# GpSimd instead of ScalarE issues layer 2's weight loads, and the fusion MLPs' inputs are fetched two images ahead: a four-layer convolution stack on one core

## The chip, the cores and the metric

The kernel runs on one core of one Trainium2 chip, in one launch. The metric is the device time of one execution in microseconds (us), given as the median of several runs. TensorE (PE), VectorE (DVE), ScalarE (ACT), GpSimd (POOL) and SyncE (SP) each run their own instructions in order; SP, ScalarE and GpSimd also issue the transfers between the DRAM and the core's own memory.

## The reference

The input x has 8 images of 384 channels of 32 x 32 pixels, float32. Four residual layers follow each other, each on a group-normalised x:

```python
x = x + L0(gn(x))   # convolutional attention: depthwise 3x3, batch norm, gelu, 8 heads
x = x + L1(gn(x))   # 4 experts of two 384x384 layers, 2 of them per pixel
x = x + L2(gn(x))   # depthwise 7x7 with reflected borders
x = x + L3(gn(x))   # three branches of MLPs and depthwise 1x1, 3x3, 5x5, mixed and projected
```

The change touches layer 2 and the beginning of layer 3. Layer 2 is one depthwise convolution:

```python
xp = jnp.pad(x, ((0, 0), (0, 0), (P, P), (P, P)), mode='reflect')     # P = 3
out = jax.lax.conv_general_dilated(xp, w, ..., feature_group_count=C) # w is (384, 1, 7, 7)
return out + b[None, :, None, None]
```

In layer 3, two of four groups of channels in each branch go through a small MLP: `h = gelu(einsum('bchw,cd->bdhw', c, mw1) + mb1)`, `y = einsum('bdhw,dc->bchw', h, mw2) + mb2`. The means of the hidden values over the image are needed for the weights that mix the three branches (the fusion).

## The kernel before, in words

**Layer 2's order of work.** The 384 channels form three tiles (ct = 0, 1, 2). A tile's input, all 8 images, lies in one buffer xt (L1836 fetches it, image by image, on SP's queue). The 7x7 convolution is done by TensorE as products with banded matrices: for each of eight column pairs c and both halves e of one, `convolve7` (L1112, L1116) runs over seven taps. So there are 48 units of work, 28 products each; the trace shows two records for each product. Every second c, ScalarE copies four full accumulator banks into `o` (`evict_slots`, L405).

**The weights' way.** The banded weights w7 lie in DRAM as 24 blocks, one for each tile and column pair (128 rows of 4256 bytes, 532 KB). `load_weights` (L1693) issues the transfer of the next block (L1704) and then two additions on GpSimd (L1708) that fold the reflected border into the band. `next_weights` (L1713) lets ScalarE spread half a block into a `wx` buffer (two activations, L1725), one half for each unit, and, when a block is used up, calls `load_weights`. Blocks land in four buffers, two tagged `w` and two tagged `xn2`; there are three `wx` buffers. `next_weights` is called right after each unit, and the order in which each engine gets its instructions is the order of the calls: the stage is scheduled by hand (`manual_schedule`). So the transfer of a block stood in ScalarE's instruction stream between the spreading of one half and the eviction or spreading that comes next. Four blocks (0, 1, 5 and 6) are issued by SP, the other 20 by ScalarE. The smaller weights of layer 3 (w35, w33) take the same way, without additions.

**Finishing a tile.** When a tile has been evicted, `finish_all` (L1874) has VectorE transpose the 8 images back (L1847), the first four into a buffer x1 and the others into four buffers y, add bias and the residual r that SP fetches (L1850, L1852), take statistics and sums, and SP store the result (L1855). For tiles 0 and 1 GpSimd copies the edges of each image (L1869). GpSimd's stream holds these copies between the additions of L1708, in the order of the calls. Near the end of tile 2 (c = 5), `fetch3` (L1905) has SP read back the stored results into the y buffers, and layer 3's first weights are loaded.

**Counting transfers.** The kernel is built by a framework that places every semaphore. In the built program SP's and ScalarE's transfers together count on eight semaphores (DMAHW0 to DMAHW7) in turn, GpSimd's on eight others (DMASW0 to DMASW7). A transfer whose semaphore was last used by a transfer that is not known to have landed waits for it before it is issued.

**Layer 3's hidden MLPs.** `hidden3(i)` (L2158) handles images 2i and 2i + 1: it takes the two input halves of each image from `hidden_in`, or calls `hidden_input` (L1928), which has GpSimd fetch them into two of the four y buffers (L1931); VectorE scales the weights (L2165), TensorE multiplies (L2171), ScalarE applies the gelu (L2179). `hidden_in` is filled for images 0 and 1 (L2070). Behind `hidden3(0)` stand GpSimd's fetches of the fusion's weights (L2190, L2191) and `windows()`, in which GpSimd fills `count` by 25 memsets (L2120) and VectorE uses it (L2138) ahead of `mean` (L2155). `hidden3(1)` to `hidden3(3)` are called between steps of the 5x5 convolution (L1969).

Of the kernel before, what the change touches and what calls it, by code (L numbers as in the profile page):

```python
# [19 lines left out]
B, C, H, W = 8, 384, 32, 32  # L20
# [33 lines left out]
K7, R7 = 7, 3  # L54
# [121 lines left out]
def conv_mixer_kernel(ctx: ExitStack, tc: tile.TileContext, a: dict, out: bass.AP):  # L176
    nc = tc.nc
# [415 lines left out]
    def layers(again, early, xst, pre_pool, pp0, pw):  # L593
# [531 lines left out]
        def begin_layer2(n, er):  # L1125

            late["xa"] = own.enter_context(
                tc.tile_pool(name="xa", bufs=1, side="right", reuse_waits="tile")
            )
            for name, bufs in (("lw", 2), ("lwx", 1), ("wx", 2)):  # L1130
                late[name] = lwpool.enter_context(
                    tc.tile_pool(name=name, bufs=bufs, side="right", reuse_waits="tile")
                )
            wxs.extend((late["lwx"], late["wx"]))
            fourth.append(er.tile([P, 2 * K7, 2, W], FP, tag="wx", name="wx4", bufs=1))
            xts.append(new_xt(late["xa"]))
            for i in range(n):
                nc.sync.dma_start(out=image_of(xts[0], i), in_=x2mem[i][0])
            for _ in range(2):
                load_weights(nc.sync)  # L1140
# [549 lines left out]
        todo_load = [(K7, ct, c) for ct in range(NC) for c in range(8)]  # L1690
        todo_load += [(n, unit, c) for unit in (1, 0) for n in KS for c in range(8)]

        def load_weights(queue=nc.scalar):  # L1693
            if not todo_load:
                return
            k, unit, c = todo_load.pop(0)
            rows, cols = 4 * k, W + (len(EDGE) if k == K7 else 0)
            n_loaded.append(c)
            if k == K7 and more_w and (len(n_loaded) - 4) % 4 > 1:
                w = more_w[0]()  # L1700
            else:
                w = late["lw"].tile([P, 4 * K7, W + len(EDGE)], FP, tag="w", name="w")
            w = w.rearrange("p r w -> p (r w)")[:, : rows * cols].rearrange("p (r w) -> p r w", w=cols)
            queue.dma_start(out=w, in_=a["w7" if k == K7 else f"w3{k}"][unit, c])  # L1704
            if k == K7:
                for c0, e0 in ((0, W), (W - R7, W + R7)):
                    o = w[:, :, c0 : c0 + R7]
                    nc.gpsimd.tensor_tensor(out=o, in0=o, in1=w[:, :, e0 : e0 + R7], op=ALU.add)  # L1708
            n = rows // WPARTS[k]
            for e in range(WPARTS[k]):  # L1710
                loaded.append(((k, unit, c, e), w[:, n * e : n * e + n, :W]))

        def next_weights():  # L1713
            if not loaded:
                return
            key, w = loaded.pop(0)
            n = w.shape[1]
            n_spread.append(key)
            if len(n_spread) == 4:
                x = fourth.pop()  # L1720
            else:
                m = len(n_spread) - (len(n_spread) > 4)
                x = wxs[m % 3 != 1].tile([P, 2 * K7, 2, W], FP, tag="wx", name="wx")
            for t in range(2):
                nc.scalar.activation(x[:, :n, t, :], w, AF.Copy, scale=parity[:, t : t + 1])  # L1725
            weights[key] = x.rearrange("p r t w -> p r (t w)")
            if key[3] == WPARTS[key[0]] - 1:
                n_placed.append(key)

                if len(n_loaded) - len(n_placed) < (4 if todo_load and todo_load[0][0] == K7 and more_w else 2):  # L1730
                    load_weights()
# [61 lines left out]
        for _ in range(2):  # L1793
            load_weights(nc.sync)
# [3 lines left out]
        def banks(turn=True):  # L1798
            return Slot(four_banks(turn))
# [38 lines left out]
        def new_y():  # L1838
            return ty.tile([P, N], FP, tag="y", name="y", bufs=4)
# [88 lines left out]
        def hidden_input(b):  # L1928
            ys = [new_y() for _ in range(2)]
            for j in range(2):  # L1930
                nc.gpsimd.dma_start(out=ys[j], in_=y2mem[b][1 + j])  # L1931
            return ys
# [57 lines left out]
        with tc.manual_schedule(engines=ORDERED | {mybir.EngineType.Pool}):  # L1990
# [79 lines left out]
            hidden_in = {b: hidden_input(b) for b in range(2)}  # L2070
# [87 lines left out]
            def hidden3(i):  # L2158


                slot, units = banks(i == 0), []
                for b in (2 * i, 2 * i + 1):
                    ys = hidden_in.pop(b, None) or hidden_input(b)
                    mw1s = fa.tile([P, 2, MR], FP, tag="mw1s", name="mw1s", bufs=2)
                    nc.vector.tensor_mul(  # L2165
                        mw1s, mw1, s3[:, 1:3, b : b + 1].to_broadcast([P, 2, MR])
                    )
                    for h in range(2):
                        ph = slot.tile([MR, HF])
                        for j in range(2):  # L2170
                            nc.tensor.matmul(  # L2171
                                ph, lhsT=mw1s[:, j], rhs=ys[j][:, h * HF : (h + 1) * HF],
                                start=j == 0, stop=j == 1,
                            )
                        units.append(ph)
                for b in (2 * i, 2 * i + 1):
                    hid = ty.tile([MR, N], FP, tag="r2", name="hid")
                    for h in range(2):
                        nc.scalar.activation(  # L2179
                            hid[:, h * HF : (h + 1) * HF], units.pop(0), AF.Gelu,  # L2180
                            bias=hbias[:, b : b + 1], accum_out=hsum[:, b, h : h + 1],
                        )
                    nc.scalar.dma_start(out=hmem[b], in_=hid)

            hidden3(0)

            fws = new_x1().rearrange("p c b h -> p (c b h)")
# [96 lines left out]
            def output_bias():  # L2284
                po = banks().tile([P, NC, B])
                for oc in range(NC):
# [8 lines left out]
                convolve3(0, 5, lambda: to.tile([P, B, H, 32], FP, tag="o", name="o")),  # L2295
                [
                    lambda: hidden3(1), None, lambda: hidden3(2), None, lambda: hidden3(3),
                    reorder, branch_mean, branch_weights,
                ],
# [272 lines left out]
```

## Time and profile before

| what | value |
|---|---|
| median of 3 runs | 3133.1 us (3128.01, 3133.1, 3138.59) |
| the profiled execution | 3131.1 us, its span 3129.4 us |
| mean granted TensorE clock | 0.979 of full speed |
| TensorE matmul / weight load busy | 95% / 55% |
| VectorE / ScalarE / GpSimd busy | 59% / 39% / 27% |
| moved by the DMA engines | 323.03 MB, 103 GB/s in the mean |
| layer 2's convolution on TensorE (L1116) | 2625.7 to 2817 us from the span's start |
| layer 3's hidden MLPs on TensorE (L2171) | 2883.9 to 2934.5 us |

Times in the profile are counted from the span's start. A row of a timeline gives start, duration, engine, line, operation, output and inputs, how many instructions are merged, and in brackets how long the engine was idle before it and what ended that. A row of the list of waits gives who waited for whom, the sum in us, how often, and the longest. L numbers are lines of the kernel before; behind L1703 the changed kernel's are one to three higher.

### The profile page before, as it was taken

What the parts mean: (1) busy time and instruction counts of PE and PEld (TensorE: products, weight loads), DVE (VectorE), ACT (ScalarE), POOL (GpSimd) and SP (SyncE); (2) the same over time, 40 slices, a digit from 0 to 9 for tenths busy, and PEclk for the clock granted to TensorE, in tenths of its full rate; (3) what the DMA queues carried; (4) which work ended last, traced back from release to release, by engine and by line L of the source; (5) the groups of instructions that cost most, each with busy time, mean ns of one, the idle gap of its engine ahead of it and who ended that gap; (6) DMA issues with size and microseconds to landing.
All of it is one profiled execution on the core that took longest, in us unless ns stands there. A gap on an engine that the chain in (4) does not pass through costs nothing. (4 is left out here: it accounts for less than half of the span.)

```text
span 3129.4 us, 45250 instructions
## 1 busy us (share of the span) xinstructions
PE 2978.0 (95%) x18280; PEld 1710.8 (55%) x18280; DVE 1857.4 (59%) x3066; ACT 1211.5 (39%) x1446; POOL 858.7 (27%) x1103
## 2 busy tenths in 40 slices
PE   4988999999999999999999999999999999886998
PEld 3765334343433434343433688788787877555543
DVE  6898344445454445444445777777777776457164
ACT  2655453544445353545433122222222223446520
POOL 2432000000000000000000577686777764111400
PEclk9999999999999999999999999999999999898999
DMA  6787102010111101110002111112112114967675
GB/s 220 262 281 287 57 23 83 23 63 23 61 46 41 63 23 63 44 63 23 31 23 94 74 41 65 57 49 85 45 45 81 52 37 161 335 204 251 232 227 187
DMA packets 89107, 323.03 MB, mean 103 GB/s; under 512 B 13608, under 2 KB 16000, under 8 KB 84664
## 3 DMA queue, kind: packets, MB, share of 16 engines
q1 hardware_dynamic: 64936, 251.71, 23.6%
q10 hardware_dynamic: 13776, 35.82, 3.7%
q0 software_dynamic: 10176, 32.51, 3.0%
q8 instruction: 146, 2.39, 0.3%
q14 instruction: 73, 0.60, 0.1%
HBM read 211.66 MB, written 111.68 MB: 103 GB/s over the span
## 5 line engine op out<-in xcount | busy, mean ns | idle before, releaser
L780 ACT ACTIVATE e<-sc 128x1024 f32<-128x1024 f32 x512 | 483.2, 1031 | 607.8 <-PE sc L773 607.7
L773 PE MATMUL sc<-qT,kT 64*128 64x512 f32 x2048 | 473.9, 602 | 0.0
L792 PE MATMUL av<-e,vT 128*64 128x512 f32 x2048 | 467.7, 599 | 0.0
L773 PEld LDWEIGHTS sc<-qT,kT 64*128 64x128 f32 x2048 | 186.8, 186 | 282.0 <-issue 231.3
L792 PEld LDWEIGHTS av<-e,vT 128*64 128x64 f32 x2048 | 135.5, 136 | 316.4 <-issue 316.4
L822 POOL DMA_DIRECT2D att<-att x45 | 23.7, 531 | 979.6 <-DVE att L817 979.6
L671 PE MATMUL sc<-y,pw 128*128 128x512 f32 x576 | 249.3, 594 | 0.0
L808 DVE LOAD_MASK_SELECT sm<-av x64 | 0.9, 14 | 417.0 <-PE av L792 417.0
L530 PE MATMUL ps<-xt,wx 64*64 64x256 f32 x3456 | 198.7, 388 | 35.2 <-DVE xt L468 20.1
L810 DVE RECIPROCAL inv<-sm 128x512 f32<-128x512 f32 x64 | 214.6, 3353 | 2.2
L1346 POOL TENSOR_TENSOR hs_sum<-hs,hs_sum 128x256 f32<-128x256 f32 (+1 forms) x225 | 209.7, 940 | 9.4
L1366 DVE TENSOR_TENSOR r<-r,p 128x256 f32<-128x256 f32 x416 | 153.2, 411 | 92.2 <-PE p L1357 90.7
L530 PEld LDWEIGHTS ps<-xt,wx 64*64 64x64 f32 x3456 | 156.8, 137 | 76.1 <-issue 39.7
L671 PEld LDWEIGHTS sc<-y,pw 128*128 128x128 f32 x576 | 108.8, 190 | 139.9 <-issue 138.5
L354 ACT ACTIVATE hs<-hs,b 128x512 f32<-128x512 f32 x135 | 88.4, 712 | 247.4 <-DVE hs L1308 246.8
L1116 PE MATMUL ps<-xt,wx 64*64 64x256 f32 (+1 forms) x2912 | 160.5, 379 | 23.8 <-ACT wx L1725 12.8
L1357 PE MATMUL p<-hs_sum,wsum 128*128 128x256 f32 x768 | 177.0, 384 | 0.0
L1308 DVE TENSOR_TENSOR hs<-p,hs_sum 128x256 f32<-128x256 f32 x270 | 114.5, 424 | 93.5 <-PE p L1299 39.0
L1299 PE MATMUL p<-forms,w 128*128 128x256 f32 x630 | 165.4, 379 | 0.0
L1323 PE MATMUL ph<-xn,w 128*128 128x512 f32 x342 | 159.3, 600 | 3.0 <-ACT xn L354 3.0
L1357 PEld LDWEIGHTS p<-hs_sum,wsum 128*128 128x128 f32 x768 | 149.2, 194 | 21.4
L1116 PEld LDWEIGHTS ps<-xt,wx 64*64 64x64 f32 x2912 | 109.2, 139 | 73.3 <-ACT wx L1725 15.1
(346 smaller groups left out, 4687.3 us busy)
## 6 DMA issues: line engine op xcount, KB each, us to landing
raw<-y SPq DMA_DIRECT2D x72, 512.0 KB
y<-raw SPq DMA_DIRECT2D x24, 1536.0 KB
x<-x SPq DMA_DIRECT2D x23, 608.0 KB
xt<-x SPq DMA_DIRECT2D x23, 608.0 KB
w<-in_w ACTq DMA_DIRECT2D x36, 384.0 KB
xn<-in_x SPq DMA_DIRECT2D x24, 512.0 KB
x<-in_x SPq DMA_DIRECT2D x16, 768.0 KB
z<-z POOLq DMA_DIRECT2D x16, 768.0 KB, 4.3
```

Of the source, the lines that this page charges most:

```text
L530: nc.tensor.matmul(ps[64 * d : 64 * d + 64, 2 * i + e, cc], lhsT=w[r, 12 * cc + 6 * e + 3 * d + k, :], rhs=xt0s[ct][r, 16 * d + 4 * u + 2 ...
L671: nc.tensor.matmul(ps[:, h, :], lhsT=w[:, ct, pair, :], rhs=y[:, ct, h * HF : (h + 1) * HF], start=ct == 0, stop=ct == NC - 1,)
L773: nc.tensor.matmul(sc[:, s, :], lhsT=kTs[b][r, pair, m * P : (m + 1) * P], rhs=qTs[b][r, pair, h * HF : (h + 1) * HF], start=True, stop=True,)
L780: nc.scalar.activation(e, sc, AF.Exp, scale=1.0 if shifted else HD**-0.5)
L792: nc.tensor.matmul(av[64 * s : 64 * s + 64, :], lhsT=vTs[0][:, m, c0 : c0 + 64], rhs=e[:, s, :], start=m == 0, stop=m == N // P - 1,)
L810: nc.vector.reciprocal(inv, sm)
L1116: nc.tensor.matmul(ps[64 * d : 64 * d + 64, 2 * i + e, c % 2, images], lhsT=w[r, d * K7 + k, :], rhs=by_slot(xts[ct])[r, 16 * d + column(c ...
L1299: nc.tensor.matmul(ps[:, :QF], lhsT=block1(PRODUCTS[n][0])[:, e], rhs=form_of(n, xn), start=True, stop=True,)
L1323: nc.tensor.matmul(ph, lhsT=w1[:, e, ct, dc * P : (dc + 1) * P], rhs=xn[:, ct, :], start=ct == 0, stop=ct == NC - 1,)
L1346: eng.tensor_add(rows_of(o, hs, s), rows_of(i, hs, s), rows_of(j, hs, s))
L1357: nc.tensor.matmul(ps[:, :QF], lhsT=block(w)[:, e], rhs=rows_of(x, hs, e), start=e == 0, stop=e == E - 1,)
L1366: nc.vector.tensor_tensor(out=o, in0=o, in1=ps[:, :QF], op=op)
```

## The change

Every w7 block that ScalarE loaded is now loaded by GpSimd; those that name SP keep it, and layer 3's weights stay with ScalarE. And after the products of image b, the inputs of image b + 2 are fetched at once, instead of at the beginning of the next call of `hidden3`.

```diff
-        def load_weights(queue=nc.scalar):
+        def load_weights(queue=None):
...
             w = w.rearrange("p r w -> p (r w)")[:, : rows * cols].rearrange("p (r w) -> p r w", w=cols)
+            queue = queue or (nc.gpsimd if k == K7 else nc.scalar)
             queue.dma_start(out=w, in_=a["w7" if k == K7 else f"w3{k}"][unit, c])
...
                 for b in (2 * i, 2 * i + 1):
-                    ys = hidden_in.pop(b, None) or hidden_input(b)
+                    ys = hidden_in.pop(b)
...
                         units.append(ph)
+                    if b + 2 < B:
+                        hidden_in[b + 2] = hidden_input(b + 2)
```

On GpSimd each of the 20 transfers now stands directly ahead of its own two additions, with one exception: block 7's stands ahead of the additions of block 6. The issue waits for ScalarE's spreading of the block that held the buffer before. The semaphores of SP's and ScalarE's remaining transfers are dealt out anew, since 20 of them left the round. The first fetch of images 2 and 3 on GpSimd moves ahead of L2190, L2191 and the memsets of L2120; the other orders stay.

## The prediction

> **What bounds the kernel now.** I read the page first. TensorE is busy nearly throughout, but the DMA row jumps to 9 in one slice, at about 2660 to 2740 us.
>
> ```profile
> PE 2978.0 (95%) x18280; PEld 1710.8 (55%) x18280; DVE 1857.4 (59%) x3066; ACT 1211.5 (39%) x1446; POOL 858.7 (27%) x1103
> ...
> DMA  6787102010111101110002111112112114967675
> ```
>
> That stretch is layer 2, whose stage runs from 2637 to 2817 us. The list of waits, cut to 2600 to 2820 us, says who waited there:
>
> ```profile
> ACT wx L1725 <- DMA r<-r: 17.5, 2, 9.1
> ...
> PE ps L1116 <- ACT wx L1725: 12.8, 5, 4.6
> ...
> ACT wx L1725 <- DMA y<-x: 11.1, 1, 11.1
> ACT wx L1725 <- DMA y<-y: 10.9, 1, 10.9
> ACT wx L1725 <- DMA fb<-in_fb: 10.2, 1, 10.2
> PE ps L1116 <- ACT o L405: 9.7, 1, 9.7
> ```
>
> ScalarE waited 17.5 + 11.1 + 10.9 + 10.2 = 49.7 us for four kinds of transfer that SP issues and that L1725 doesn't read. The timeline of ScalarE shows where one such wait sits:
>
> ```profile
> 2662.47 0.33 ACTq L1704 DMA_DIRECT2D xn<-in_w  x1
> ...
> 2667.64 1.23 ACT L1725 ACTIVATE wx<-xn,parity 128x448 f32<-128x448 f32 x2 [2.08 <-PE ps L1116]
> 2678.56 0.33 ACTq L1704 DMA_DIRECT2D xn<-in_w  x1
> 2679.02 1.23 ACT L1725 ACTIVATE wx<-w,parity 128x448 f32<-128x448 f32 x2 [10.15 <-DMA fb<-in_fb]
> ```
>
> The idle time lies ahead of a weight load (L1704 at 2678.56), not ahead of the spreading (L1725) it is booked to. In the built kernel's instruction list the reason is plain: the transfers of SP and ScalarE share eight counters in turn, and this load must first see the SP transfer ahead of it on its counter land. So ScalarE stands, the weights spread behind the load come late, and TensorE runs dry:
>
> ```profile
> 2664.27 12.51 PE L1116 MATMUL ps<-xt,wx 64*64 64x256 f32 x224
> 2680.30 33.71 PE L1116 MATMUL ps<-xt,wx 64*64 64x256 f32 x560 [3.52 <-ACT wx L1725]
> ...
> 2718.57 8.78 PE L1116 MATMUL ps<-xt,wx 64*64 64x256 f32 x112 [4.56 <-ACT wx L1725]
> ...
> 2801.40 5.26 PE L1116 MATMUL ps<-xt,wx 64*64 64x256 f32 x56 [9.73 <-ACT o L405]
> ```
>
> I number the 24 loads of w7 by order (load k holds column pair k % 8 of channel tile k // 8); each is spread in two halves, units 2k and 2k + 1 of TensorE, 56 matmul records each. The row at 2664.27 gives four undisturbed units in 12.51 us, 3.13 us each; the next ten took 3.37 each, and the two from 2718.57 took 4.39, at a granted clock of 0.64 to 0.67 in the slices of 5 us from 2715 to 2725.
>
> **Part one: loads 2 to 4 and 7 to 23 issued by GpSimd.** ScalarE loses 20 issues of 0.33 us and the waits ahead of loads 10, 15, 16 and 23. The fifth stall (10.92 us, to 2797.86) stands before the first w35 load, which stays on ScalarE behind the same SP transfer of fetch3, so it stays too; only its time can move. What lies on the path up to unit 31 (the end of tile 1): idle TensorE of 3.52 + 4.56 + 1.98 us, and slow units of 10 x 0.24 + 2 x 1.26 = 4.9 us; together 15.0 us.
>
> Against it: load 4 now stands behind the copies of L1018 on GpSimd, 0.6 us later than ScalarE's 2645.70; its additions, the memsets of L1081 and the eviction that waits for them follow, and with unit 7 already waiting 0.34 us I take 0.9 us. So unit 31 comes at most 14.1 us earlier.
>
> What is late next? Tile 1's finishing on VectorE must end before fetch3 lands, and fetch3 releases the w35 load, the eviction (L405) behind it and unit 44. Its start, at 2752.83, had two conditions that fell together:
>
> ```profile
> 2751.65 0.75 POOL L1708 TENSOR_TENSOR w<-w 128x84 f32<-128x84 f32 x2 [5.23 <-DMA w<-in_w]
> 2752.34 0.32 POOL L1869 COPY edges<-y 128x8 f32<-128x8 f32 x2
> ```
>
> ```profile
> 2752.83 4.62 DVE L1847 STREAM_TRANSPOSE x<-o 128x1024 f32<-128x1024 f32 x4 [17.84 <-POOL edges L1869]
> ```
>
> The eviction of tile 1 ended at 2752.73. And the last of the eight transposes takes over the y buffer of tile 0's image 7, whose edge copies (L1869, 2752.34) stand on GpSimd behind load 20's additions. That queue is what the change lengthens. Before, a load was in flight while GpSimd waited for an earlier one. Now GpSimd issues a load, waits for it to land, adds (0.75 us), copies edges if due, and only then issues the next; queued behind each landing are the next load, the edge copies, and through them VectorE.
>
> So GpSimd's line has to be added up. Load 7 waits for the spreading that ended at 2654.72, 0.9 us later now; landed and added, it lets load 8 go at about 2660.8. From there to image 7's copies lie thirteen loads, 8 to 20. Nine of them (8 to 16) fall into the saturated stretch, four after it. Landing there: ScalarE's ten loads 9 to 18 took 5.05 to 8.55 us from issue to the additions, 7.0 in the mean (2662.47 to 2671.02 is the longest). GpSimd's own loads of y (512 KB, L1931, at a DMA share of 0.5 to 1.0) landed in 3.8, 5.1 and 7.0 us, lowest, median, highest. I take 6.5: nearer to ScalarE's mean, which is the same transfer in the same stretch, and a little lower because two of mine are never in flight together. In the quiet stretch ScalarE's took 3.7; I take 4.3 for the dearer issue (0.53 against 0.33 us) and y's 3.8 at best. With 0.75 of additions and 0.15 to wake: 9 x 7.4 + 4 x 5.2 + 8 x 0.33 of copies = 90.0 us, so the copies end at 2750.8. One transpose (1.2 us) on, VectorE's L1852 starts at 2752.0 where it started at 2761.88: 9.9 us earlier. The cap of 14.1 would be reached with 6.0 us per landing. The weights themselves stay in time: load 14 would be added at 2660.8 + 7 x 7.4 = 2712.6, and unit 28, at 2654.77 + 0.9 + 21 x 3.13 = 2721.4, needs it a spreading (1.25 us) ahead, at 2720.1.
>
> From there the finishing takes as long as before, less some waits for r (0.88 + 0.75 + 1.85 us), whose SP transfers also lose the loads from their counters; bounds 0 and 3.5, I take 1.0 because VectorE's own work sets most of the pace. Unit 44 and all behind it in layer 3 then come 10.9 us earlier, for that chain (fetch3, w35, eviction, unit 44) keeps its order.
>
> The Trainium skill speaks against a gain of this kind: the page DMA: Bandwidth & Descriptors, section Issuing engines are not separate DMA queues, says that issuing from more engines only saves the sequencer's issue time. By that the sum would be nought for part one, since 20 x 0.33 us of ScalarE are covered; the trace so far disagrees, as the 49.7 us are waits of a queue and no issue time. That case is the third rival.
>
> **Part two: inputs two images ahead.** It does not fetch earlier. In the rows of the trace image 2's loads already wait only for TensorE's reading of image 0 (L2171), because four y buffers hold two images:
>
> ```profile
> 2884.83 0.88 POOL L2120 MEMSET count<- 128x1 f32 x25
> 2887.03 0.54 POOL L1931 DMA_DIRECT2D y<-y  x1 [1.31 <-PE ps L2171]
> ...
> 2890.46 0.53 POOL L1931 DMA_DIRECT2D y<-y  x1 [2.05 <-PE ps L2171]
> ```
>
> ```profile
> 2887.90 0.21 DVE L2138 TENSOR_TENSOR kcount<-ksum,count 128x50 f32<-128x50 f32 x1
> ```
>
> What moves is that L2190, L2191 and the memsets of count (L2120) now stand behind image 3's loads. These end at 2891.85; 1.15 us of issues and 0.88 of memsets put count at 2893.9, where VectorE's L2138 ran at 2887.90. From L2138 to the scaled weights of image 2 (L2165) VectorE needs 2.6 + 0.3 us, so they come at 2896.9, and TensorE's hidden matmuls, which began at 2895.48, wait 1.4 to 1.5 us. TensorE is busy all of 2885 to 2935, so nothing absorbs it: +1.5 us. fw1, also later, isn't read before 2944.
>
> **Sum.** -9.9 - 1.0 + 1.5 = -9.4 us on the profiled execution of 3131.1 us (span 3129.4 and 1.7 around it): 3121.7. The median of the runs is 2.0 higher, so 3123.7 there.
>
> **Rivals.** *GpSimd becomes the pace.* If landings in the saturated stretch take as long as ScalarE's longest or more, the copies, and then the weights, come late. Break-even is at 7.5 us per landing (copies at 2760.2); 8.6 makes it 9.4 us slower, and load 14 would by then be added at 2660.8 + 7 x 9.5 = 2727.3, behind unit 28's need. For it: 8.55, 8.18 and 8.02 us are in the rows, plus 0.2 of dearer issue. Against: the mean is 7.0, with pairs in flight. Price at 9.3 us: 9 x 2.8 = 25 us more on the line than I summed, so +16 us, 3149.
>
> *VectorE holds GpSimd up.* Of GpSimd's additions of 0.40 us a few took 1.37 to 1.40, one at 2701.73 while VectorE ran L1852. If the issue and an addition of the six loads between 2692 and 2735 each lose 0.97 us, the line grows by 11.6 us, and the sum becomes +2.2 us: 3135. Against: the y load issued at 2855.36 during L1852 took 0.63 us where 0.53 is usual. The skill's same page, section SWDGE vs HWDGE vs iDMA, says that the descriptors GpSimd writes lie in SBUF, where VectorE's two-port modes lock it out, and that ScalarE's loads are immune; only the 0.1 us of that row bears it out here.
>
> *The wait moves and nothing is gained.* Only issue time is saved, or the load's wait was for its buffer and is repeated on GpSimd: part one 0, part two +1.5, 3134.6. Against: loads 19 to 22, with the same buffers, issued without such a wait.
>
> **How the numbers follow.** A measurement of this kernel can tell about 0.3%, 9.4 us. My forecast sits on that edge: landings of up to 6.5 us give more, 6.5 to 7.5 less. Forecast (gain of 3 to 16 us) 0.66, of which 0.50 above 9.4; GpSimd the pace 0.18, of which 0.16 beyond +9.4; VectorE 0.09; nothing gained 0.07. Faster 0.50, same 0.34, slower 0.16. The low end is the cap, 14.1 + 3.5 - 1.5 = 16.1 us, less some of the runs' spread (5 us): 3114. The high end takes in a landing of 8.5 us, ScalarE's mean plus 1.5 (9 x 2.0 = 18 us more, so +8.6): 3141.
>
> **What would show it.** Right: the four ScalarE waits of 8 to 11 us ahead of L1705 gone, one left before w35; image 7's copies of tile 0 near 2750; VectorE's second set of transposes ending near 2752; count's memsets at about 8 us after image 0's matmuls. Wrong: w landing in over 7.5 us from GpSimd, TensorE waiting for L1726 in tile 1, or that one remaining stall not ending earlier.

## The result, and the profile after

The changed kernel takes 3125.51 us in the median of 9 runs (3122.39 to 3131.36), the kernel before 3132.43 in 9 runs beside it (3125.64 to 3138.59). The ratio is 0.9982 with a 95% interval of 0.9973 to 0.999: a gain of 5.6 us by the ratio and of 6.9 us between the medians, small, but above nothing by the interval. The span of the profiled execution went from 3129.4 to 3123.3 us. All medians here and below are of undisturbed runs; the kernel before with its first w35 load moved had two more, of 3506.43 and 5527.2 us at a granted clock of 0.846 and 0.708, which are left out.

In what follows, the list of waits is always that of 2600 to 2820 us. In lines of the changed kernel, L1705 is the weight load, L1709 its additions, L1726 the spreading, L1848 the transposes, L1853 bias and residual, L1870 the edge copies.

The page first. TensorE's busy time hardly changes, and in the DMA row the slice of layer 2 has an 8 where the 9 was, and three slices on there is a 7 for a 6:

```profile
PE 2972.1 (95%) x18280; PEld 1719.4 (55%) x18280; DVE 1858.2 (59%) x3066; ACT 1211.7 (39%) x1446; POOL 869.6 (28%) x1123
...
DMA  6787102010111101110002211112112114867775
```

The list of waits of the changed kernel (who waited for whom, sum, times, longest):

```profile
POOL w L1709 <- DMA w<-in_w: 55.6, 14, 7.8
...
ACT wx L1726 <- POOL w L1709: 24.3, 5, 14.2
...
ACT wx L1726 <- DMA y<-y: 19.9, 1, 19.9
...
PE ps L1116 <- ACT o L405: 10.0, 1, 10.0
...
ACT o L405 <- DVE y L1848: 5.3, 1, 5.3
DVE y L1848 <- POOL edges L1870: 4.9, 2, 3.7
...
PE ps L1116 <- ACT wx L1726: 2.7, 1, 2.7
```

Of the four kinds of transfer that held ScalarE up, only y<-y, ahead of the first w35 load, is left (19.9 us, 10.9 before), and TensorE's waits for spread weights fell from 12.8 to 2.7 us. New are two: VectorE waits for edge copies in the middle of its transposes, and ScalarE's eviction for VectorE. And one has grown: ScalarE's spreading waits for GpSimd's additions (w 24.3 us, xn 6.1). Without the first of these waits, which lies ahead of the stage (14.2 us, 14.3 before), that is 16.2 us where it was 1.0.

TensorE's timeline says the same. From 2664.28 on it runs 29 units without a gap, where it had gaps of 3.52, 4.56 and 1.98 us. A unit takes 89.35 / 29 = 3.08 us, and the granted clock, 0.91 from 2660 to 2700 us and 0.87 from 2700 to 2740 us before, is 1.00 in both. So the slow units of the prediction are gone together with the gaps. But unit 44 (2793.08) still stands behind the eviction:

```profile
2664.28 89.35 PE L1116 MATMUL ps<-xt,wx 64*64 64x256 f32 x1624
2756.32 15.58 PE L1116 MATMUL ps<-xt,wx 64*64 64x256 f32 x280 [2.69 <-ACT wx L1726]
...
2781.61 1.45 PE L279 MATMUL ps<-mv,gmatB 128*128 128x8 f32 x6 [9.39 <-DVE mv L1859]
2793.08 6.21 PE L1116 MATMUL ps<-xt,wx 64*64 64x256 f32 x56 [10.02 <-ACT o L405]
...
2813.75 10.74 PE L1970 MATMUL ps<-x,wx 64*64 64x128 f32 x280 [4.11 <-DVE x L1925]
```

GpSimd's line is the one the prediction added up: issue, wait, additions, edge copies, next issue. It reached the copies of image 7 of tile 0 at 2751.65:

```profile
2735.11 0.75 POOL L1709 TENSOR_TENSOR xn<-xn 128x84 f32<-128x84 f32 x2 [5.27 <-DMA xn<-in_w]
...
2746.94 0.56 POOL L1705 DMA_DIRECT2D w<-in_w  x1
2750.96 0.74 POOL L1709 TENSOR_TENSOR w<-w 128x84 f32<-128x84 f32 x2 [3.45 <-DMA w<-in_w]
2751.65 0.31 POOL L1870 COPY edges<-y 128x8 f32<-128x8 f32 x2
```

VectorE's last transpose of tile 1 follows these copies by 0.03 us, and the finishing starts 8.7 us earlier than before (2753.16 for 2761.88):

```profile
2738.97 4.62 DVE L1848 STREAM_TRANSPOSE x<-o 128x1024 f32<-128x1024 f32 x4 [4.87 <-issue]
...
2747.03 1.25 DVE L1848 STREAM_TRANSPOSE y<-o 128x1024 f32<-128x1024 f32 x1 [1.19 <-POOL edges L1870]
2751.99 1.25 DVE L1848 STREAM_TRANSPOSE y<-o 128x1024 f32<-128x1024 f32 x1 [3.72 <-POOL edges L1870]
2753.16 1.24 DVE L1853 SCALAR_TENSOR_TENSOR x<-x,b,r 128x1024 f32<-128x1024 f32 x1
```

ScalarE's timeline holds the two places that matter later. The eviction of tile 1 (2737.03) stands behind a spreading that waited for GpSimd's additions, and the w35 load (2789.54) comes at the end of 19.86 us:

```profile
2735.90 1.23 ACT L1726 ACTIVATE wx<-xn,parity 128x448 f32<-128x448 f32 x2 [4.41 <-POOL xn L1709]
2737.03 1.84 ACT L405 COPY o<-ps 128x2048 f32<-128x2048 f32 x1
...
2789.54 0.33 ACTq L1705 DMA_DIRECT2D w<-in_w  x1
2790.05 1.23 ACT L1726 ACTIVATE wx<-w,parity 128x448 f32<-128x448 f32 x2 [19.86 <-DMA y<-y]
2791.18 1.84 ACT L405 COPY o<-ps 128x2048 f32<-128x2048 f32 x1
```

Part two is seen on GpSimd, VectorE and TensorE. The memsets of `count` come 9.0 us after the first hidden products (2878.46), where they came 0.9 us after them in the kernel before, and TensorE waits ahead of image 2:

```profile
2881.56 0.59 POOL L1932 DMA_DIRECT2D y<-y  x1 [7.01 <-PE ps L2172]
...
2887.43 0.88 POOL L2121 MEMSET count<- 128x1 f32 x25
```

```profile
2888.35 0.21 DVE L2139 TENSOR_TENSOR kcount<-ksum,count 128x50 f32<-128x50 f32 x1 [6.11 <-POOL count L2121]
...
2890.95 0.52 DVE L2166 TENSOR_TENSOR mw1s<-mw,s 128x144 f32<-128x144 f32 x2
```

```profile
2891.36 7.06 PE L2172 MATMUL ps<-y,mw1s 128*72 128x512 f32 x16 [1.27 <-ACT wx L1726]
```

TensorE's row names a spreading of ScalarE, but that had ended at 2890.50. What ended last is VectorE's scaling of the weights (L2166, the first of two, at about 2891.25), and VectorE had stood 6.11 us for `count`.

### The profile page after: what moved, and what is told of

The parts are those of the page before. It is cut to its first block, busy times and chain, and to the rows that moved or that the text cites. A ratio compares the mean times of both kernels' runs of the same rounds, so it can differ in the third digit from the quotient of the medians.

```text
span 3123.3 us, 45274 instructions
## 1 busy us (share of the span) xinstructions
PE 2972.1 (95%) x18280; PEld 1719.4 (55%) x18280; DVE 1858.2 (59%) x3066; ACT 1211.7 (39%) x1446; POOL 869.6 (28%) x1123
## 3 DMA queue, kind: packets, MB, share of 16 engines
q8 instruction: 146, 2.39, 0.3%
## 5 line engine op out<-in xcount | busy, mean ns | idle before, releaser
L530 PEld LDWEIGHTS ps<-xt,wx 64*64 64x64 f32 x3456 | 158.6, 139 | 74.1 <-issue 39.3
L1116 PE MATMUL ps<-xt,wx 64*64 64x256 f32 (+1 forms) x2912 | 153.8, 369 | 13.9 <-ACT o L405 10.0
L1346 POOL TENSOR_TENSOR hs_sum<-hs 128x256 f32<-128x256 f32 (+1 forms) x135 | 132.8, 1013 | 58.7 <-ACT hs L354 50.5
```

The source lines that it names most:

```text
L530: nc.tensor.matmul(ps[64 * d : 64 * d + 64, 2 * i + e, cc], lhsT=w[r, 12 * cc + 6 * e + 3 * d + k, :], rhs=xt0s[ct][r, 16 * d + 4 * u + 2 ...
L1116: nc.tensor.matmul(ps[64 * d : 64 * d + 64, 2 * i + e, c % 2, images], lhsT=w[r, d * K7 + k, :], rhs=by_slot(xts[ct])[r, 16 * d + column(c ...
L1346: eng.tensor_add(rows_of(o, hs, s), rows_of(i, hs, s), rows_of(j, hs, s))
```

## The experiments

My theory was that of the prediction: ScalarE's stalls are waits on shared counters, the moved loads take four of five away, GpSimd's line and the fifth stall give part of it back, and part two is a cost. The first four kernels take the change apart and test the fifth stall; the other four test GpSimd's line and put together what helped.

One measure is used throughout beside the time: the stretch on TensorE from the first 7x7 product behind L1100 to the first product of layer 3's convolution (before: 2664.27 to 2821.12). It leaves out what happens earlier, which moves some starts by up to 5 us from profile to profile. It scatters too: it differs by 3.2 us between the kernel before and part two alone, which are the same there. Differences of that size in one profile decide nothing alone, nor is the profiled execution always a middle one (3116.89 us at a median of 3121.96 with the copies on VectorE). The kernels were timed in three jobs, each beside the kernel before, whose median differs by up to 1.7 us between jobs; a difference of medians from two jobs can be off by that. So the fourth column gives how far each lies under the kernel before of its own job.

| kernel | stretch, us | median, us | under before, us | ratio to before, 95% |
|---|---|---|---|---|
| before | 156.85 | 3132.43, 3130.74, 3132.13 (three jobs) | | |
| changed | 149.47 | 3125.51 | 6.9 | 0.9982 (0.9973 to 0.999) |
| part one alone | 147.58 | 3124.16 | 6.6 | 0.9987 (0.9975 to 0.9999) |
| part two alone | 153.66 | 3131.23 | -0.5 | 1.0005 (0.9994 to 1.0015) |
| changed, first w35 load on GpSimd | 140.21 | 3114.47 | 16.3 | 0.9951 (0.9935 to 0.9966) |
| before, first w35 load on GpSimd | 149.17 | 3123.34 | 7.4 | 0.9972 (0.9962 to 0.9983) |
| changed, edge copies on VectorE | 146.63 | 3121.96 | 10.2 | 0.9971 (0.996 to 0.9983) |
| changed, additions one load later | 140.62 | 3116.44 | 15.7 | 0.9953 (0.9939 to 0.9967) |
| part one, w35 load, copies on VectorE | 136.97 | 3113.23 | 18.9 | 0.9947 (0.9934 to 0.996) |
| part one, w35 load, additions later | 129.87 | 3107.02 | 25.1 | 0.9925 (0.9912 to 0.9938) |

### Part one alone

```diff
-                    ys = hidden_in.pop(b)
+                    ys = hidden_in.pop(b, None) or hidden_input(b)
...
-                    if b + 2 < B:
-                        hidden_in[b + 2] = hidden_input(b + 2)
```

> Part one alone: the w7 loads on GpSimd, hidden_input called where it was before. Theory (part two is a cost of 1.4 us and the gain is part one's): TensorE's wait of 1.27 us ahead of the hidden matmuls of image 2 vanishes, count's memsets come back to about 6.5 us after the hidden matmuls of image 0 began, and the time is 1.4 us under the changed kernel's, about 8.3 us under the kernel before (ratio 0.9973). Rival (fetching two images ahead is worth something): as slow as the changed kernel or slower, a ratio of 0.9978 or more, and a new wait for y at L2171.

The time doesn't settle it. The median is 1.35 us under the changed kernel's, as expected, but that one is from another job; under the kernel before of its own job part one alone lies 6.6 us, the changed kernel 6.9. The ratio's interval (0.9975 to 0.9999) takes in the rival's 0.9978 and leaves the theory's 0.9973 just outside. So by the time alone the cost of part two is not shown. The trace shows it where it arises: TensorE's wait ahead of image 2's products is gone, they follow the row at 2882.55 without idle time:

```profile
2882.55 4.61 PE L1970 MATMUL ps<-xt,wx 64*64 64x256 f32 x80
2887.08 7.09 PE L2172 MATMUL ps<-y,mw1s 128*72 128x512 f32 x16
```

There is no new wait for y at L2172. The 6.5 us that I gave for the memsets was a wrong figure: they come 0.9 us after the first hidden products began (2876.39 and 2875.53), just as before the change.

### Part two alone

The edit is the second half of the change, without the first.

> Part two alone: loads as before on ScalarE, inputs of the fusion MLPs asked for two images ahead. Theory: nothing changes up to the first hidden matmuls (the stage's stalls of 10.15, 11.08, 17.5 and 10.92 us on ScalarE all there), then the memsets of count come about 3 us later than before and TensorE waits some 1.4 us ahead of image 2: +1.4 us on the kernel before (ratio 1.0005, inside what the runs can tell). Rival (earlier loads are worth something, or the wait is absorbed later): 0 or a gain, no idle TensorE ahead of image 2.

The four kinds of stall are all there (10.2 us for fb, 9.6 for y<-x, 9.1 for r, 8.8 for y<-y; a second of 8.40 us, ahead of load 16, is booked to TensorE in this profile and to r in the kernel before). Image 2 then waits as in the changed kernel, and as it doesn't in the run above:

```profile
2895.72 7.06 PE L2171 MATMUL ps<-y,mw1s 128*72 128x512 f32 x16 [1.28 <-ACT wx L1725]
```

The ratio 1.0005 lies on the expected value, but its interval takes in 1, so the size rests on the trace alone: 1.27 and 1.28 us with part two, none without, on an engine that is busy right after.

### The first w35 load on GpSimd, in the changed kernel and in the kernel before

```diff
-            queue = queue or (nc.gpsimd if k == K7 else nc.scalar)
+            queue = queue or (nc.gpsimd if k == K7 or len(n_loaded) == 25 else nc.scalar)
```

> The changed kernel with the first w35 load (load 25 in all) also issued by GpSimd; all other loads of w35 stay on ScalarE. Theory (ScalarE's 19.86 us, and through them unit 44, are that load's wait for the second transfer of fetch3 on its shared counter, no need of ScalarE's own): the wait vanishes, the eviction behind it runs near 2771 us instead of 2791, unit 44 starts right behind the gn matmuls at about 2783.3 instead of 2793.1, layer 3's convolution (L1970) starts 9 to 13 us earlier than 2813.8, and with 2 us given back later the time is 7 to 11 us under the changed kernel, 14 to 18 under the kernel before (ratio about 0.995). Rival A (VectorE's finishing of tile 1 sets unit 44 anyway, the wait for the load only lies beside it): unit 44 within 2 us of 2793 and no gain. Rival B (fetch3 itself, landed near 2789.5, sets layer 3's start through L354): unit 44 early, but L1970 starts less than 5 us earlier, gain 3 to 5 us.

The theory held in each place. GpSimd issues the load at 2777.39, where ScalarE could only at 2789.54: the load needs nothing that came later than that. ScalarE's wait is gone, and unit 44 follows the group norm's products at once:

```profile
2777.39 0.56 POOL L1705 DMA_DIRECT2D w<-in_w  x1 [0.20 <-POOL edges L1870]
```

```profile
2773.36 1.23 ACT L1726 ACTIVATE wx<-w,parity 128x448 f32<-128x448 f32 x2 [1.92 <-PE ps L1116]
2774.49 1.84 ACT L405 COPY o<-ps 128x2048 f32<-128x2048 f32 x1
```

```profile
2781.99 1.45 PE L279 MATMUL ps<-mv,gmatB 128*128 128x8 f32 x6 [8.52 <-DVE mv L1859]
2783.37 5.42 PE L1116 MATMUL ps<-xt,wx 64*64 64x256 f32 x56
...
2803.30 10.31 PE L1970 MATMUL ps<-x,wx 64*64 64x128 f32 x280 [4.16 <-DVE x L1925]
```

The eviction ran at 2774.49 instead of the 2771 that I expected, because TensorE's own products were the next to wait for; it costs nothing. Both rivals fell: unit 44 did not wait for VectorE until 2793, and layer 3 began 10.5 us earlier. The time is 11.0 us under the changed kernel's median, or 9.4 when each is set against the kernel before of its own job (16.3 and 6.9). So the load's wait was not for its buffer or its data. Nor was it for an earlier transfer of ScalarE's, which in the changed kernel issues none in the stage up to then. That leaves what the built program says, a counter shared with a transfer of SP's fetch3, and the trace books the wait to that (y<-y).

The same line was put into the kernel before, with its w7 loads left on ScalarE:

> The kernel before with one load moved: the first w35 load issued by GpSimd, all loads of w7 on ScalarE as before. Theory (the fifth stall is of the same kind as the four that the change removes, and the change left it): ScalarE's 10.92 us for y<-y vanish, the other four stalls stay, unit 44 starts some 9 us earlier than 2801.4, and the time is 6 to 9 us under the kernel before, as much as the whole change brings, by one moved load. Rival (unit 44 is held by VectorE's finishing and the gn matmuls in the kernel before, the load's wait lies beside it): within 2 us of the kernel before.

```profile
2796.17 1.84 ACT L405 COPY o<-ps 128x2048 f32<-128x2048 f32 x1
```

```profile
2798.07 4.96 PE L1116 MATMUL ps<-xt,wx 64*64 64x256 f32 x56 [2.25 <-ACT o L405]
```

The wait for y<-y is gone, the others stay (10.9 us for fb, 9.4 for y<-x and 18.7 for r), and the eviction now waits for nothing but its order. The stage began 4.1 us late in this profile; counted from the first row of the stretch, unit 44 comes 7.4 us earlier, where I expected some 9. The stretch is 7.7 us shorter, and the median 7.4 us under the kernel before. One load moved brings about what the change brings with twenty (6.9).

### Edge copies on VectorE

```diff
             for g in range(2):
-                nc.gpsimd.tensor_copy(
+                nc.vector.tensor_copy(
```

> The changed kernel with the edge copies of layer 2 (L1870) on VectorE instead of GpSimd, so that no transpose of tile 1 has to wait for copies that stand behind GpSimd's loads. Theory (GpSimd's line to image 7's copies sets the start of tile 1's finishing): VectorE's waits of 1.19 and 3.72 us for edges vanish, the first L1853 of tile 1 starts near 2749.3 instead of 2753.2 (eight transposes of 1.2 us behind 2739.0), ScalarE's wait of 5.27 us for the o buffer and TensorE's 2.69 us behind it shrink by 3 to 4 us; VectorE pays some 0.12 us for each of the 16 copies of a tile, 2 us ahead of unit 44, so unit 44 comes about 2 us earlier than 2793.1 and the time is 1 to 2 us under the changed kernel, less than these runs can tell: the places in the trace decide. Rival (the eviction of tile 1 or the r transfers set that start, GpSimd lies beside it): L1853 at 2753 or later and unit 44 some 2 us later, by the added copies.

VectorE's waits for edges are gone, and its eight transposes run through:

```profile
2738.86 4.62 DVE L1848 STREAM_TRANSPOSE x<-o 128x1024 f32<-128x1024 f32 x4 [8.29 <-ACT o L405]
2743.40 4.58 DVE L1848 STREAM_TRANSPOSE y<-o 128x1024 f32<-128x1024 f32 x4
2747.91 1.24 DVE L1853 SCALAR_TENSOR_TENSOR x<-x,b,r 128x1024 f32<-128x1024 f32 x1
```

They start no earlier than in the changed kernel, though this profile's stage began 4.7 us earlier: the eviction ahead of them (2736.98) stood behind a spreading that waited 4.80 us for GpSimd's additions.

```profile
2735.85 1.23 ACT L1726 ACTIVATE wx<-xn,parity 128x448 f32<-128x448 f32 x2 [4.80 <-POOL xn L1709]
```

So GpSimd's line holds the finishing at a second place, which the copies alone don't free. Counted from the first row of the stretch, L1853 comes only 0.5 us earlier than in the changed kernel, and unit 44 2.2 us. GpSimd's additions were also dearer: four pairs took 1.14 to 1.72 us, where those of the changed kernel from load 8 on took 0.74 to 0.89 with one of 1.25; no run shows why. The stretch is 2.8 us shorter, somewhat more than expected and within the scatter, and the ratio's interval overlaps that of the changed kernel: the time shows no worth of the copies.

### Additions one load later

```diff
             queue.dma_start(out=w, in_=a["w7" if k == K7 else f"w3{k}"][unit, c])
+            while add_later:
+                add_edges(add_later.pop(0))
             if k == K7:
-                for c0, e0 in ((0, W), (W - R7, W + R7)):
...
+                add_later.append(w)
+                if len(n_loaded) < 8 or len(n_loaded) == 24:
+                    add_edges(add_later.pop(0))
```

`add_edges` holds the two additions as they were.

> The changed kernel with GpSimd's order changed for loads 7 to 22: it issues load k + 1 first and only then waits for load k and adds its edge columns, so two loads are in flight and the line of issue, landing and additions is broken up. Theory (the serial line of 7 us landings is what was left of the 14.1 us cap): edge copies of image 7 well before 2748, the first L1853 of tile 1 near 2749.3 instead of 2753.2, TensorE's 2.69 us at 2756.32 gone, unit 44 and all behind it 3 to 4 us earlier, time 2 to 4 us under the changed kernel. Rival A (two loads in flight each land as much later, as ScalarE's did at 7.0 us with pairs in flight): the copies no earlier than 2750, no change. Rival B (additions that come a load later hold up the spreading): new TensorE waits for L1726 behind L1709 in tile 1 or 2, slower than the changed kernel.

The theory's direction held, and the effect was more than twice its size: stretch 8.9 us shorter, median 9.1 us under the changed kernel. GpSimd now waits for its buffers (34.6 us in eleven waits for ScalarE's spreading, which follows TensorE), and TensorE runs 34 units without a gap:

```profile
2664.28 104.73 PE L1116 MATMUL ps<-xt,wx 64*64 64x256 f32 x1904
...
2785.56 4.85 PE L1116 MATMUL ps<-xt,wx 64*64 64x256 f32 x56 [9.18 <-ACT o L405]
```

```profile
2735.75 0.32 POOL L1879 COPY edges<-y 128x8 f32<-128x8 f32 x2
2737.10 0.55 POOL L1712 DMA_DIRECT2D xn<-in_w  x1 [1.03 <-ACT wx L1735]
```

```profile
2733.44 1.84 ACT L405 COPY o<-ps 128x2048 f32<-128x2048 f32 x1
```

```profile
2737.13 4.61 DVE L1857 STREAM_TRANSPOSE x<-o 128x1024 f32<-128x1024 f32 x4
2741.67 4.57 DVE L1857 STREAM_TRANSPOSE y<-o 128x1024 f32<-128x1024 f32 x4
2746.17 1.24 DVE L1862 SCALAR_TENSOR_TENSOR x<-x,b,r 128x1024 f32<-128x1024 f32 x1
```

Both places can be read off. The last copies of tile 0 are done at 2736.1, so the 1.19 + 3.72 us of waiting for them fall away. And the eviction of tile 1 runs at 2733.44 instead of 2737.03, as no spreading ahead of it waits for additions; the transposes start 1.84 us earlier, with VectorE's own work on tile 0 right ahead of them. Together 6.75 of the 6.99 us by which L1853 (here L1862) is earlier. I had counted the first place alone. The remaining 1.4 us of unit 44's length (4.85 for 6.21 us) came on top. Rival A was right in one thing: with two loads in flight the median landing of GpSimd's twenty loads rose from 5.4 to 6.5 us. But no single landing holds up the line any more. Rival B fell: TensorE has no wait behind the additions.

### The combinations

Both leave part two out and put the first w35 load on GpSimd; the first has the copies on VectorE, the second the later additions.

> Part one without part two, the first w35 load on GpSimd, and the edge copies on VectorE. Theory: the terms add up: 10.5 us of the first w35 load (what unit 44's side of that run showed), 1.3 of part two, 2 of GpSimd's line less the copies: 12 to 14 us under the changed kernel, 19 to 21 under the kernel before (ratio about 0.9935). Rival (with the load's wait gone VectorE's finishing sets unit 44, so copies on VectorE cost their 2 us in full): no better than 0.9948, the moved w35 load and part one alone.

The median lies 12.3 us under the changed kernel's and 18.9 under that of the kernel before, at the foot of what the theory gave. The ratio 0.9947 is the rival's edge (0.9948), and its interval (0.9934 to 0.996) takes in the theory's 0.9935 and the 0.9951 of the moved w35 load alone: the copies on VectorE cannot be told from nothing. TensorE had no gap up to 2769.86 and then waited 11.51 us for VectorE, where it waited 8.52 us with the w35 load alone moved.

> Part one without part two, the first w35 load on GpSimd, and the additions one load later in GpSimd's order. Theory: 10.5 + 1.3 + 3 to 4 us: 14 to 16 us under the changed kernel, 21 to 23 under the kernel before (ratio about 0.993), the fastest of all. Rival (later additions hold up the spreading, or two loads in flight each land later): no better than 0.9948.

A little more than the theory gave, and the fastest of all: 25.1 us under the kernel before in the same job, 18.5 under the changed kernel's median (18.2 with each against its own job). The stretch is 27.0 us shorter than before. Unit 44 has no wait of its own left; ahead of it TensorE waits 3.65 us for VectorE's statistics:

```profile
2663.83 104.73 PE L1116 MATMUL ps<-xt,wx 64*64 64x256 f32 x1904
...
2772.53 1.45 PE L279 MATMUL ps<-mv,gmatB 128*128 128x8 f32 x6 [3.65 <-DVE mv L1868]
2773.90 5.30 PE L1116 MATMUL ps<-xt,wx 64*64 64x256 f32 x56
...
2793.70 10.26 PE L1979 MATMUL ps<-x,wx 64*64 64x128 f32 x280 [4.14 <-DVE x L1934]
```

## Why the prediction was right, and where its steps were off

The forecast was 3123.7 us, within 3114 to 3141; measured were 3125.5. It is a little less close than that looks: the gain forecast was 9.4 us, and 6.9 were measured. The chain it named is the chain the trace shows, but for what holds the eviction of tile 1. Step by step, in the profiled executions:

| step | forecast | measured |
|---|---|---|
| ScalarE's waits ahead of loads 10, 15, 16, 23 | gone | gone |
| GpSimd's landings in the saturated stretch (loads 8 to 16) | 6.5 us | 7.0 (3.99 to 9.43) |
| landings behind it (17 to 20) | 4.3 us | 4.6 |
| copies of image 7 | end 2750.8 | end 2751.96 |
| first L1853 of tile 1 | -9.9 us | -8.7 |
| waits for r in tile 1 | -1.0 | -0.6 |
| unit 44 | -10.9 | -8.3 |
| part two at image 2 | +1.4 to +1.5 | +1.3 to +1.4 |
| span | -9.4 | -6.1 |

**GpSimd's line** was the right term with the right size within 1.2 us, a part of which is luck: from load 8 to the copies it took 92.8 us instead of 90.0, because the landings came out at ScalarE's mean of 7.0 and not at 6.5, but load 8 went at 2659.12 instead of 2660.8. Behind it 0.4 us of the r waits, and 0.9 between the last store of tile 1 and the landing of fetch3, were missing at unit 44; the latter no run took apart. Unit 44 itself took 6.21 us for 5.26, which left 7.4 us at layer 3's start. At the first hidden products 5.5 were left; on the way image 7 of tile 2 waited 3.36 us for r where it had waited 2.39. Part two took its 1.4 us, which left 4.1, and 2.0 came back between there and the end. These small terms are of the scatter that the stretch shows between like kernels, so I would not give any of them a cause.

**The cap** is the step that failed, though its number seemed to fit. I let the eviction of tile 1 follow unit 31 and capped it at 14.1 us; it came 13.9 us earlier, but for another reason: it stood behind a spreading that waited 4.41 us for GpSimd. With the additions taken off the line it came 17.4 us earlier (2750.89 to 2733.44). Of the 3.3 us between cap and possible, 0.9 were load 4's delay, which was not paid (TensorE's row starts at 2664.28, and at 2664.27 before), and 1.2 come from the undisturbed unit, 89.35 / 29 = 3.08 us instead of 3.13 over 24 units; the rest is open. So the prediction saw GpSimd's line at one of the two places where it acts, the copies ahead of the transposes, and missed the additions ahead of the spreading and, through ScalarE's order, ahead of the eviction.

**The fifth stall** was seen to stay, with its reason, but nothing was made of it: moving that one load proved worth more than the change. ScalarE came to it earlier and waited longer, 19.86 for 10.92 us, so that of the four stalls removed on the way only as much was kept as fetch3 itself came earlier.

**The rivals.** That nothing is gained because issuing elsewhere saves only issue time fell: the twenty issues of 0.33 us were covered, and the time fell by 5.6 to 6.9 us. The Trainium skill's page DMA: Bandwidth & Descriptors, section Issuing engines are not separate DMA queues, says that starting transfers from several engines saves just the sequencer's time. The single w35 load bounds that more sharply: one issue of 0.33 us moved, 9.4 to 11.0 us gained, so here the rule leaves out the waits that stand in front of an issue. GpSimd as the pace did not reach its break-even of 7.5 us per landing in the mean, though four of the nine landings lay above it; but GpSimd set the start of tile 1's finishing, at a cost of 7.0 us there against the run with later additions. VectorE holding GpSimd up: between 2692 and 2735 us the issues took 0.55 to 0.56 us and a load's two additions 0.74 to 0.89; nothing like the price I gave.

## What to carry to other kernels

A transfer's issue in an engine's stream can wait for more than its buffer: look at which counter it takes and which transfer had that counter before, and at what stands behind it on the engine; here a load of 0.33 us of issue held the eviction behind it for 19.86 us. When a load moves to another engine, add up that engine's whole line, landing waits included, and follow everybody who waits for work queued on it, not only the load's own users. A consumer of a transfer that is put right behind its issue on the same engine makes the line serial; one step of distance between the two was worth about 9 us here.

## What the runs showed that I had not expected

That the landing of one 532 KB block differs as much within one stretch as it does, 3.99 to 9.43 us from issue to additions on GpSimd at a DMA share of 0.92, with only one block in flight beside SP's transfers. And that the two remedies add up so far: with each kernel set against the kernel before of its own job, 9.4 us for the w35 load, 8.8 for the additions and 1.3 for part two (by its place in the trace) make 19.5, and the three together gave 18.2.
